# Attention 1 of a fused transformer layer: both diagonal blocks of four heads on the token side, sums copied by ScalarE, products on GpSimd

## The chip, the cores and the metric

The kernel runs on one core of a Trainium2 chip. The metric is device microseconds of that core, median of several runs: 4908.79 us before the change (10 runs, 4905.26 to 4916.34). The core has five engines that each work through their own instructions in order: TensorE (PE; its weight loads are shown as PEld), VectorE (DVE), ScalarE (ACT), GpSimd (POOL) and SyncE (SP). Semaphores order them among each other. DMA transfers are issued here from SP and from POOL.

## The reference, cut to what matters

The layer is an attention over channels, a layer norm, a second attention over the sequence with a mixture of experts, and more norms. The change touches the first attention alone:

```python
Q = (x @ Wq + bq).reshape(b, s, H, C) * inv_sqrt_c      # H = 16, C = 64
K = (x @ Wk + bk).reshape(b, s, H, C)
V = (x @ Wv + bv).reshape(b, s, H, C)
scores = jnp.einsum('bshq,bshk->bshqk', Q, K)
scores = jnp.where(mask, -inf, scores)                   # mask: k > q
w = jax.nn.softmax(scores, axis=-1)
attn = jnp.einsum('bshqk,bshk->bshq', w, V).reshape(b, s, HID) @ Wo + bo
x = _layernorm(x + attn)
```

There are 8 x 1024 = 8192 tokens of 256 features. For each token and head the scores are the outer product of two vectors of 64 numbers, a 64 x 64 square of which the lower triangle counts. A softmax runs along its rows, and the result is multiplied by the 64 values of V. No two tokens meet in it.

## The kernel before, in words

**Tiles and cycles.** `phase_a` works on 64 tiles of 128 tokens. A tile has eight cycles c = 0 to 7: cycles 0 to 3 take the tile's first 64 tokens, 4 to 7 the other 64, and each of the four takes four of the 16 heads. The loop `for t in range(NT + 1)` (L762) writes the instructions of all engines out by hand, cycle by cycle; the dictionaries `between`, `after`, `fill_a` and `fill_b` (L714 to L735) say which work of the tile before ("-"), this one ("") or the next one ("+") is put between the cycle's parts. Each engine keeps that order.

**Scores on PE.** `scores(t, c, which)` (L376) makes score blocks by matmuls over tiles R (q and the row maxima, spread block-diagonally) and L (k and constants), so that a matmul gives q·k minus the row's maximum. `which` 0 and 1 take two heads each: the first 32 columns against all 64 rows. `which` 2 takes all four heads: the last 32 columns against the last 32 rows. Ahead of them four bfloat16 matmuls (L388) put the mask in. Each call fills two PSUM tiles `pair` of 128 x 1024, out of three, and ACT takes their exponential into a tile `e` (L416).

**Sums on PE.** `sums(t, c, which)` (L420) multiplies `e` by V, spread with columns of ones, so that numerators and denominators come out together: L430 for the first 32 columns, L439 for the last 32. Both calls of a cycle use the one PSUM bank `sum`; it is copied to the tile S (L451) by ACT for the first two heads and by DVE for the other two. After every second cycle eight POOL DMAs (L461) carry S to `nd`, which has one row per token.

**The token side.** In cycles 3 and 7, the last four heads, `scores` has no call with `which` 2. The last 32 x 32 block of these heads is done with one token per partition: `token_scores` multiplies k by q on DVE (L497), subtracts the row maximum on POOL (L498) and masks there by affine_select (L500); `token_exp` is on ACT; `token_sums` (L521 to L523) is a row sum, a product with v and another row sum on DVE. The six `pieces` are strips of 8 rows, 256 to 512 elements per partition, one begun in each of cycles 0 to 5 and finished in the next. `token_v` (L465) makes v for it by a projection of its own, at the end of cycle 7.

**Operands.** `extrema` and `maxima` give the row maxima: two running scans of k, two products with q (L343, L344) and a maximum, all on DVE. `build(t, r)` copies q and maxima to R by eight POOL DMAs (L357) and k to L by 16 SP DMAs (L363). It is called in cycles 0, 2, 4 for the pair of cycles after the next, and in cycle 6 for the next tile. There are two R and two L. `gather` writes a one-element `event` on POOL (L371) after waiting for these transfers, and the score matmuls wait for the event.

**After the sums.** `divide` (L525) makes a quarter of the attention output: reciprocal of the denominators (L533) and a product (L534), two quarters in cycle 7 and two in cycle 1 of the next tile; the last adds the token side's part. `turn` transposes it in cycles 4 and 5 of the next tile, `output` multiplies by Wo in cycles 6 and 7, its second half ending with the sum r (L569) on DVE and the norm's statistics. All projections, `turn` and `output` share one PSUM bank `ps`.

The order of one cycle, in the loop:

```python
if live and c < len(pieces):
    token_scores(t, c)
if live:
    scores(t, c, 0 if short else 2)      # short: c % 4 == 3
if c % 2 == 1 and (live and c < 7 or more):
    gather((c + 1) // 2 % 4)
if before is not None:
    sums(*before, 1)
...
if live and c % 2 == 0 and c < 6:
    build(t, c // 2 + 1)
```

then `fill_a`, `scores(t, c, 0)` where the cycle isn't short, `token_exp(t, c - 1)`, `between`, `scores(t, c, 1)`, `sums(t, c, 0)`, `fill_b`, `token_sums(t, c - 1)` and `after`.

## Time and profile before

| | |
|---|---|
| median of 10 runs | 4908.79 us |
| the profiled execution | 4919.86 us, span 4918.1 us |
| TensorE clock granted, mean of the span | 0.982 |
| exponentials of attention 1 (L416), first to last start | 40.1 to 4187.1 us |
| L416, ACT, 128 x 1024 | 2816 times, mean 1021 ns |
| L451, copy of sums by DVE / by ACT | 512 times each, 691 / 592 ns |
| L461 and L357, POOL DMA issues | 2048 times each, 492 and 483 ns |
| L498, POOL subtraction on the token side | 384 times, mean 1009 ns |
| L533, DVE reciprocal | 256 times, 1740 ns |

A row of the profile names the line, the engine, the operation and what it writes and reads, then how often, for how long, and how long the engine was idle before it and what ended that. `s<-k,qm` is the product on the token side, `R<-qm` the fetch of operands, `nd<-S` the way back of the sums. In the order of time each row has its start in us from the span's start and its duration in us; rows of one kind that follow each other are merged (x8). A duration of PE is that of a pipelined matmul: the distance from one start to the next says what it costs.

### The profile page before, as it was taken

What the parts mean: (1) busy time and instruction counts of PE and PEld (TensorE: products, weight loads), DVE (VectorE), ACT (ScalarE), POOL (GpSimd) and SP (SyncE); (2) the same over time, 40 slices, a digit from 0 to 9 for tenths busy, and PEclk for the clock granted to TensorE, in tenths of its full rate; (3) what the DMA queues carried; (4) which work ended last, traced back from release to release, by engine and by line L of the source; (5) the groups of instructions that cost most, each with busy time, mean ns of one, the idle gap of its engine ahead of it and who ended that gap; (6) DMA issues with size and microseconds to landing.
All of it is one profiled execution on the core that took longest, in us unless ns stands there. A gap on an engine that the chain in (4) does not pass through costs nothing.

```text
span 4918.1 us, 173591 instructions
## 1 busy us (share of the span) xinstructions
PE 4691.3 (95%) x70872; PEld 3047.9 (62%) x70872; DVE 3767.6 (77%) x7390; ACT 3503.9 (71%) x4759; POOL 2990.6 (61%) x5670
## 2 busy tenths in 40 slices
PE   8999999999999999999999999999999998888785
PEld 4666666666666666666666666666666665555563
DVE  6777777777777777877777787777777776577778
ACT  5777777777777777777777777777777777444334
POOL 5666666666666666666666666666666665132346
PEclk9999999999999999999999999999999999999987
DMA  2212222221222222212222122222222222133443
GB/s 78 49 48 51 48 49 48 49 50 48 51 50 48 51 47 50 51 47 50 49 48 51 48 50 49 49 51 48 49 49 49 51 49 68 49 77 83 130 150 116
DMA packets 521795, 285.98 MB, mean 58 GB/s; under 512 B 373921, under 2 KB 439841, under 8 KB 520993
## 3 DMA queue, kind: packets, MB, share of 16 engines
q1 hardware_dynamic: 378466, 113.23, 11.8%
q0 software_dynamic: 139264, 159.69, 10.3%
q8 instruction: 554, 9.08, 0.8%
q10 hardware_dynamic: 3264, 1.97, 0.2%
q14 instruction: 247, 2.02, 0.1%
HBM read 72.90 MB, written 33.85 MB: 22 GB/s over the span
## 4 chain that ended last, share of the span: by engine, by line
PE 40%; DVE 7%; ACT 3%; DMA 2%; issue 1%; POOL 1%; SPq 0%; ACTq 0%; POOLq 0%; DVEq 0%
PE pair L400 10%; PE sum L430 9%; PE pair L388 3%; PE sum L439 3%; PE ps L290 2%; PE ps L323 2%; PE ps L279 2%; PE ps L564 2%; ACT s L959 1%; DMA w<-in_w 1%; ACT e L416 1%; PE fill L1017 1%; PE fill L890 1%; PE ps L546 1%; DVE n L1252 1%
## 5 line engine op out<-in xcount | busy, mean ns | idle before, releaser
L416 ACT ACTIVATE e<-pair 128x1024 f32<-128x1024 f32 x2816 | 2729.8, 1021 | 957.1 <-PE pair L400 950.4
L400 PE MATMUL pair<-R,L 32*128 32x128 f32 (+1 forms) x28672 | 1497.9, 332 | 21.6 <-POOL event L371 21.3
L461 POOL DMA_DIRECT2D nd<-S x2048 | 992.4, 492 | 530.5 <-DVE S L451 459.1
L430 PE MATMUL sum<-e,V 128*32 128x256 f32 x16384 | 1241.3, 386 | 13.0 <-ACT S L451 1.8
L400 PEld LDWEIGHTS pair<-R,L 32*128 32x128 f32 x28672 | 1138.8, 186 | 71.5 <-POOL event L371 29.6
L357 POOL DMA_DIRECT2D R<-qm x2048 | 973.2, 483 | 59.3 <-issue 40.4
L451 DVE COPY S<-sum 128x512 f32<-128x512 f32 x512 | 354.0, 691 | 653.2 <-PE sum L439 543.4
L498 POOL TENSOR_TENSOR s<-s,qm 128x512 f32<-128x512 f32 (+2 forms) x384 | 387.6, 1009 | 575.2 <-DVE s L497 572.1
L439 PE MATMUL sum<-e,V 128*32 128x128 f32 x12288 | 617.6, 273 | 0.0
L430 PEld LDWEIGHTS sum<-e,V 128*32 128x32 f32 x16384 | 412.3, 109 | 330.7 <-ACT S L451 74.3
L439 PEld LDWEIGHTS sum<-e,V 128*32 128x32 f32 x12288 | 399.6, 110 | 264.3 <-issue 0.9
L388 PE MATMUL pair<-late,sel 32*128 32x256 bf16 (+1 forms) x5632 | 484.2, 307 | 7.2 <-ACT e L416 7.2
L311 DVE COPY V<-vT 32x128 f32<-32x128 f32 (+1 forms) x2048 | 458.7, 224 | 27.1
L388 PEld LDWEIGHTS <-sel 32*128 32x128 bf16 x5632 | 154.9, 91 | 492.4 <-issue 466.3
L533 DVE RECIPROCAL att<-nd 128x256 f32<-128x256 f32 x256 | 445.5, 1740 | 13.7 <-DMA nd<-S 9.5
L451 ACT COPY S<-sum 128x512 f32<-128x512 f32 x512 | 303.2, 592 | 0.8 <-PE sum L439 0.8
L500 POOL TENSOR_SCALAR_AFFINE_SELECT s<-s 128x128 f32<-128x128 f32 (+1 forms) x384 | 276.1, 719 | 28.2
L279 PE MATMUL ps<-wk,xT 128*128 128x512 f32 x512 | 257.5, 626 | 11.9 <-DMA wk<-in_Wk 10.6
L290 PEld LDWEIGHTS ps<-xT,wv 128*128 128x128 f32 x2048 | 238.2, 191 | 45.3 <-issue 25.8
L290 PE MATMUL ps<-xT,wv 128*128 128x128 f32 x2048 | 262.6, 281 | 1.6 <-DVE qm L324 0.8
L323 PE MATMUL ps<-wq,xT 128*128 128x512 f32 x512 | 257.4, 626 | 5.3 <-DVE k L280 5.3
L564 PE MATMUL ps<-wo,attT 128*128 128x256 f32 x1024 | 255.0, 392 | 0.7 <-ACT attT L547 0.7
(244 smaller groups left out, 5327.5 us busy)
## 6 DMA issues: line engine op xcount, KB each, us to landing
R<-qm POOLq DMA_DIRECT2D x2048, 32.0 KB, 2.2
nd<-S POOLq DMA_DIRECT2D x2048, 32.0 KB, 1.9
L<-k SPq DMA_DIRECT2D x4088, 8.0 KB
rows_d<-yx SPq DMA_DIRECT2D x32, 512.0 KB
xT<-in_xT SPq DMA_DIRECT2D x64, 128.0 KB
xr<-in_x SPq DMA_DIRECT2D x64, 128.0 KB
x_d<-x1o SPq DMA_DIRECT2D x64, 128.0 KB
w<-in_w SPq DMA_DIRECT2D x32, 256.0 KB
```

The costliest lines, as they stand in the source:

```text
L290: nc.tensor.matmul(ps[:, i * P : (i + 1) * P], w["v"][:, c, ch * P : (ch + 1) * P], xT_of[t][:, c, :], start=c == 0, stop=c == DC - 1,)
L311: nc.vector.tensor_copy(V[32 * aa : 32 * aa + 32, :, qd // 2, :, aa, 0:4], src[32 * qd : 32 * qd + 32, :n, ww, :, aa, :],)
L357: moved.append((None, nc.gpsimd.dma_start(R[:, b, s, b, :], q[:, b, s, cols])))
L388: nc.tensor.matmul(bank[u].rearrange("p (n i) -> p n i", i=n)[:, :, 0:32], sel[pr].rearrange("p a j -> p (a j)"), late[pr, None, :].to_bro ...
L400: one = nc.tensor.matmul(bank[u][:, x * 4 * n : (x + 1) * 4 * n].rearrange("p (b i) -> p b i", i=n), Lt[pr, 2 * (h0 + h) + jb].rearrange(" ...
L416: nc.scalar.activation(e, pair[i], AF.Exp)
L430: nc.tensor.matmul(dst[32 * u : 32 * u + 32], Vs[ww][:, h0 + h, u, :], e0[u // 2][:, u % 2, x * 256 : (x + 1) * 256].rearrange("p (b i) -> ...
L439: nc.tensor.matmul(dst[32 * u : 32 * u + 32, :, 32:], Vs[ww][:, H1 + h0 + h, u, :], e1[u // 2][:, u % 2, h * 128 : (h + 1) * 128].rearrang ...
L451: (nc.vector.tensor_copy if which else nc.scalar.copy)(S[:, :, at : at + 2, :].rearrange("p b h i -> p h b i"), ps.rearrange("p (h b i) -> ...
L461: nc.gpsimd.dma_start(tok[:, b, s, (h0 - G) * C1 : (h0 + G) * C1], Sx[:, 4 if s else b, b, :])
L498: nc.gpsimd.tensor_tensor(s, s, m, ALU.subtract)
L533: nc.vector.reciprocal(att[:, cols], nd[:, 1, cols])
```

## The change

In cycles 3 and 7 ("full" now) both diagonal 32 x 32 blocks of the four heads go to the token side, and PE keeps only the square between them, last 32 rows against first 32 columns, which needs no mask: one `scores` call (L411 in the new file) without mask matmuls and one `sums` call of 128-column matmuls for all four heads.

The eight triangles of 32 rows are cut into squares of 16, 8 and 4 and triangles of 4. Five pieces take the place of six: two of squares of 16 (1024 elements per partition each), one of squares of 8 (1024), one of triangles of 4 (1024, masked by adding a constant tile `above` on POOL) and one of squares of 4 (512). They begin in cycles 0, 1, 2, 4 and 5, and each is finished in the cycle after. Their row sums go to `part` and `corner`, and the last quarter of `divide` has four adds in place of one.

All sums are copied from PSUM by ACT. The products of the maxima go to POOL (`products`, in cycles 4 and 5), the maximum stays on DVE, in cycles 5 and 6. `residual_bias` goes to POOL. `token_v` is two transposes of the projected v and an ACT copy, in cycle 6. The tiles `e` are six of a list instead of eight of a pool, S is two fixed tiles, and the scratch of dynamic DMAs is 2048 bytes instead of 4096.

```diff
-    HT, BI = 4, 8
-    pieces = [(0, 0, 4), (1, 0, 4), (2, 0, 2), (2, 2, 2), (3, 0, 2), (3, 2, 2)]
+    HT, BI = 4, 4
+    TC = HT * C1
+    pieces = [(16, 0, 4), (16, 4, 4), (8, 0, 16), (0, 0, 64), (4, 0, 32)]
+    begin = [(0,), (1,), (2,), (), (3,), (4,), (), ()]
+    finish = [(), *begin[:7]]
...
+        def products(t, half):
...
+            nc.gpsimd.tensor_tensor(hi, hi, qm[:, 0, cols], ALU.mult)
+            nc.gpsimd.tensor_tensor(lo, lo, qm[:, 0, cols], ALU.mult)
+
         def maxima(t, half):
...
-            nc.vector.tensor_tensor(hi, hi, qm[:, 0, cols], ALU.mult)
-            nc.vector.tensor_tensor(lo, lo, qm[:, 0, cols], ALU.mult)
             nc.vector.tensor_tensor(hi, hi, lo, ALU.max)
...
-            for u in range(4):
+            full = c % 4 == 3
+            for u in range(0 if full else 4):
...
-            jb = 0 if which < 2 else 1
+            jb = 0 if which < 2 or full else 1
...
-            (nc.vector.tensor_copy if which else nc.scalar.copy)(
-                S[:, :, at : at + 2, :].rearrange("p b h i -> p h b i"),
-                ps.rearrange("p (h b i) -> p h b i", h=2, b=4),
+            n, i0 = (4, 32) if full else (2, 0)
+            nc.scalar.copy(
+                S[:, :, at : at + n, i0:].rearrange("p b h i -> p h b i"),
+                ps.rearrange("p (h b i) -> p h b i", h=n, b=4),
             )
...
+            nc.vector.tensor_tensor(s, k, q, ALU.mult)
+            nc.gpsimd.tensor_tensor(s, s, m, ALU.subtract)
+            if pieces[n][0] == 0:
+                nc.gpsimd.tensor_tensor(s, s, above[:, None, :, :].to_broadcast(shape), ALU.add)
...
+            nc.vector.tensor_reduce(rows[1], s, AX.X, ALU.add)
+            nc.vector.tensor_tensor(s, s, v, ALU.mult)
+            nc.vector.tensor_reduce(rows[0], s, AX.X, ALU.add)
...
-                nc.vector.tensor_tensor(late, late, state["nt", t], ALU.add)
+                own = nd[:, :, cols]
+                nc.vector.tensor_tensor(own, own, corner, ALU.add)
+                for w, p in part.items():
+                    rows = own.rearrange("p s (b z i) -> p s b z i", z=2, i=w)[:, :, :, 1, :]
+                    nc.vector.tensor_tensor(rows, rows, p.rearrange("p s (b i) -> p s b i", i=w), ALU.add)
...
-            nc.vector.tensor_tensor(xr, xr, bo, ALU.add)
+            nc.gpsimd.tensor_tensor(xr, xr, bo, ALU.add)
...
-            4: [("+", maxima, 0)],
-            5: [("+", maxima, 1), ("-", residual_bias)],
-            6: [("+", spread_v, 0, 0)],
+            4: [("+", products, 0)],
+            5: [("+", maxima, 0), ("+", products, 1), ("-", residual_bias)],
+            6: [("+", maxima, 1), ("+", spread_v, 0, 0)],
...
-                short = c % 4 == 3
-                if live and c < len(pieces):
-                    token_scores(t, c)
+                full = c % 4 == 3
+                for n in begin[c][:1] if live else ():
+                    token_scores(t, n)
                 if live:
-                    scores(t, c, 0 if short else 2)
+                    scores(t, c, 2)
...
-                if live and 0 < c <= len(pieces):
-                    token_sums(t, c - 1)
+                for n in finish[c][:1] if live else ():
+                    token_sums(t, n)
...
-    nc = bacc.Bacc("TRN2", target_bir_lowering=False, num_devices=1, dynamic_dma_scratch_size=4096)
+    nc = bacc.Bacc("TRN2", target_bir_lowering=False, num_devices=1, dynamic_dma_scratch_size=2048)
```

## The prediction

> **What bounds the kernel now.** I read the page first, then busy time by window, groups by form, one tile in order of time, and the waits.

> ```profile
> span 4918.1 us, 173591 instructions
> PE 4691.3 (95%) x70872; PEld 3047.9 (62%) x70872; DVE 3767.6 (77%) x7390; ACT 3503.9 (71%) x4759; POOL 2990.6 (61%) x5670
> ...
> 2000.00:3000.00 1000.00, 993.48 (x16384) 639.96 (x16380) 787.20 (x1463) 775.16 (x930) 653.80 (x1272) 1.00 0.21 49
> ```

> The last line is one millisecond inside attention 1: PE 99.3% busy at full clock, DVE 79%, ACT 78%, POOL 65%. TensorE sets the pace. The event ahead of each pair of cycles occurs 124 times from 1013.2 to 2997.9 us, four per tile, so a tile takes 1984.7/123 x 4 = 64.5 us. But one chain that feeds PE has almost no slack, which one tile in order of time shows (start, duration):

> ```profile
> 2043.73 0.41 DVE L569 TENSOR_TENSOR r<-ps,xr 128x256 f32<-128x256 f32 x1
> ...
> 2047.04 0.41 DVE L497 TENSOR_TENSOR s<-k,qm 128x256 f32<-128x256 f32 x1
> ...
> 2063.71 0.55 DVE L497 TENSOR_TENSOR s<-k,qm 128x384 f32<-128x384 f32 x1
> 2064.34 0.84 POOL L498 TENSOR_TENSOR s<-s,qm 128x384 f32<-128x384 f32 x1 [5.56 <-DVE s L497]
> 2065.74 3.84 POOL L461 DMA_DIRECT2D nd<-S  x8
> 2069.57 3.80 POOL L357 DMA_DIRECT2D R<-qm  x8
> ...
> 2076.47 0.09 POOL L371 MEMSET event<- 1x1 f32 x1
> ...
> 2076.82 1.27 PE L400 MATMUL pair<-R,L 32*128 32x128 f32 x32
> ```

> Cycle 2 of this tile starts on PE at 2061.70, cycle 4 at 2076.54. The operands R of cycles 4 and 5 are fetched by POOL in cycle 2, behind the token subtraction of cycle 2, which itself waits for the DVE product k·q at 2063.71. The event comes at 2076.47 and PE's matmuls follow at 2076.82: already now just in time. Whatever makes k·q of cycle 2 later moves the event by as much.

> ```profile
> POOL s L498 <- DVE s L497: 140.9, 46, 5.6
> POOL nd L461 <- DVE S L451: 104.6, 16, 8.8
> POOL event L371 <- DMA R<-qm: 26.1, 17, 3.1
> ```

> Of the waits in the same millisecond (total, times, longest), POOL's largest is for that product, up to 5.6 us.

> **What PE saves.** By start-to-start times, a scores call with 256-column matmuls is 1.09 us, one with 128 columns 1.21 (0.22 of it the mask matmuls), a sums call without a second block 1.00, with it 1.44. Cycles 3 and 7 lose 2 x 1.09 + 2 x 1.00 = 4.18 us and get one unmasked scores call (1.0, the 32-matmul row) and one sums call of 32 matmuls over 128 columns. Eight such take 0.22 to 0.33 us in L439's rows: 0.9 to 1.3, I take 1.0. token_v's projection (0.65) becomes two transposes (0.3, half of four in 0.6). Together 2 x 2.18 + 0.35 = 4.7 us: PE needs 59.8 us a tile, if fed.

> **What the others get.** By these rows of the same millisecond:

> ```profile
> L533 DVE RECIPROCAL att<-nd 128x256 f32<-128x256 f32 x60 | 104.4, 1740 | 0.7
> L498 POOL TENSOR_TENSOR s<-s,qm 128x512 f32<-128x512 f32 x47 | 50.2, 1068 | 41.2 <-DVE s L497 40.7
> L497 DVE TENSOR_TENSOR s<-k,qm 128x512 f32<-128x512 f32 x47 | 32.2, 685 | 0.2
> ...
> L497 DVE TENSOR_TENSOR s<-k,qm 128x256 f32<-128x256 f32 x15 | 6.2, 415 | 0.0
> ```

> - DVE token work: 0.415 at 256 elements, 0.685 at 512, so an estimated 1.22 at 1024; the reduces have the same line (0.411, 0.686). Four operations on 4 x 1024 + 512 elements are 22.3 us against 14.3 now. Three adds more in divide and a wider one: 0.6 + 3 x 0.4 = 1.8 against 0.4. Gone: its eight S copies, 8 x 0.69 = 5.5; four products 2 x (1.07 + 0.81) = 3.8; vt 0.3; xr 0.5. Net -0.7: DVE's total hardly moves, its order does.
> - POOL: 0.63 at 256, 1.07 at 512, so 1.94 at 1024. Subtractions 8.8 against 6.0, the new add 1.9, products 4 x 1.07 = 4.3, xr 0.6, no masks by affine_select (-4.3): +5.3 on 42 us. Products come after R in cycle 4 and after the event in cycle 5, xr behind them; ahead of the next issues that leaves about 3 us free, so I price their place at 0, at most their 2.1 + 2.1 + 0.6 if that cover goes. DVE's maximum in cycle 5 now waits for the first products, some 14 us into cycle 4 (two token operations 3.9, nd 3.95, R 3.8, products 2.1). Behind it on DVE stands the copy that frees the projection bank for the turn; PE has 2.5 us of scores and sums before it wants that bank, which covers the delay: 0, at most 1 us.
> - ACT: four exponentials of 0.97 fewer, six copies of 0.59 more, token exponentials 4.9 (0.82 per 1000 elements and 0.21 fixed, from 420 and 631 ns) against 3.4, vt 0.4: 49.8 becomes about 51.5 of 59.8. A sum's copy now stands behind two exponentials; nd waits for it, but the subtraction holds POOL longer. The token exponential of 1.05 in cycles 1, 2, 3, 5 may hold the sum bank some 0.2 us each: hidden while PE waits anyway, else up to 0.8.
> - SP's L issues and the number of POOL DMAs stay. The DMA scratch is halved: 139264 packets over 4096 transfers are 34 each, and 2.2 us to landing at 0.48 an issue mean about 5 in flight. I take 0; if the half allowed only half of these, issues would space at 0.96 and the 16 in the chain would cost 7.7 us a tile. No row points there.

> **The chain, in us after r** (r waits for the end of output's second half, now the last thing of cycle 7):
> 1. r, statistics, second divide: 3.1 (2107.93 to 2111.04 in the next tile). k·q of cycle 0: 1.2, at 4.3.
> 2. POOL subtraction 1.94, at 6.35; eight nd issues 3.95, at 10.3; landing 1.9, at 12.2. DVE meanwhile: V copies 2.2 + 1.8, k 0.6, k·q of cycle 1, all done by 12.0 even if held 1.9 by the subtraction.
> 3. divide of the third quarter needs that nd: 2.2, at 14.4; second k copy 0.6, at 15.0.
> 4. POOL: eight R to 14.1, subtraction of cycle 1 to 16.05. The four adds of divide's last quarter wait for it (below): 16.05 + 1.8 = 17.85; reciprocal and product 2.2, at 20.05.
> 5. token sums of cycle 1, 3 x 1.22: 23.7. Then only k·q of cycle 2: 24.9. Before, it ended 20.5 after r.
> 6. POOL: subtraction, at 26.95; nd 3.85, R 3.8, at 34.6; landing 2.2 (once 3.5, from 2088.8 to the event at 2092.3), event and PE 0.2: 37.0. Before: 33.1.
> 7. PE from there to the end of output: 8.1 + 8.8 + 8.5 + 4.4 = 29.8 for cycles 4 to 7, and 0.1 to r.

> Sum 66.9 us, a closed loop, against PE's 59.8. PE alone would be there 59.8 - 29.9 = 29.9 us after r, so it waits some 7 us at cycle 4; a second wait, for the event of cycle 0, is 1 to 2 us and hidden by the first. The tile shown took 64.2 (r at 2043.73 and 2107.93), the mean 64.5; with the same 0.3 for what disturbs a tile now and then: 67.2. So +2.7 us on some 63 tiles, +170; the first tile has no divide and saves 4.7. The profiled run took 4919.86, 11 above the median, so 4920 + 165 = 5085 like it and **5075** on the median's scale. DMA landing (1.9 to 3.5) and step 4 bound this loop at 65.6 to 69.5: 4980 to 5225.

> **The lock in step 4.** [...]

> ```profile
> 2088.79 1.67 DVE L343 TENSOR_TENSOR qm<-qm 128x512 f32<-128x512 f32 x1
> ...
> 2088.84 1.06 POOL L498 TENSOR_TENSOR s<-s,qm 128x512 f32<-128x512 f32 x1
> ```

> 1.67 us where L345, of the same size, has 0.69: it ended 0.56 after POOL. The adds would be free at 15.0 and are held to 16.05. [...] Without any lock it would be 1.05 x 63 less, 5010. [...]

> **Rivals.**
> - PE stays the bound (faster). 64 x 4.7 = 301 us less, 4608. For it: the 99.3%. Against it: step 6 would have to end at 29.9, with k·q of cycle 2 done 17.8 us after r, which leaves 5.6 after step 2's landing for steps 3 to 5, whose DVE rows alone are 11.7. Break-even is 64.5 - 29.9 = 34.6 at step 6.
> - The loop is there but shorter by 3 to 6 us (a landing that isn't waited for, shorter wide operations): 60.5 to 64 us a tile, 4660 to 4880.
> - POOL's and DVE's lock or the 4-wide rows cost more: 3 to 5 us on cycles 4 to 7, where DVE has some 0.5 us to spare before r. 70 to 72 us: 5260 to 5390. For it: L343's row; against it: DVE waits for nd there anyway.

> **How the numbers follow.** Loop as summed 0.70 (4980 to 5240), dearer 0.08, shorter loop 0.08, PE-bound 0.11, no change 0.03 (0.2%, 10 us, is about what can be told apart). So slower 0.78, same 0.03, faster 0.19. The range leaves out the PE-bound case, the lower part of the shorter loop and the upper part of the dearer: 4850 to 5250; the likeliest case's own is 4980 to 5225.

> **What would show it.** Tile period near 67; PE waiting some 7 us per tile for the event ahead of cycle 4, PE's share near 89% in the middle; DVE products of 1024 near 1.22, POOL's near 1.94; POOL's longest wait for k·q of cycle 2. Wrong if that event comes before PE gets there, or if 1024-wide rows are far from these.

## The result, and the profile after

The changed kernel takes 5640.17 us (median of 8 runs, 5633.86 to 5658.82) against 4909.23 for the kernel before, run beside it: a ratio of 1.1493 (1.1483 to 1.1503). It is slower, as predicted, but by 731 us, not by 166, and outside the range. By the sums r, of which there is one per tile, a tile took (4208.2 - 164.1) / 63 = 64.19 us before (first and last of them) and (4948.5 - 183.2) / 63 = 75.64 us now: 11.45 more, and 63 times that is 721 of the 731 us. The last of these intervals is short, 20.5 and 21.7 us, since its tile has none after it to prepare; over 32 tiles in the middle the mean is 64.5 us before, which is the prediction's figure, and 76.4 now.

First the page of the kernel after (engine shares, and three groups with their idle time and what ended it):

```profile
PE 4658.0 (82%) x69720; PEld 3131.5 (55%) x69720; DVE 4162.2 (74%) x6430; ACT 3567.3 (63%) x4887; POOL 3425.5 (61%) x5609
...
L411 PE MATMUL pair<-R,L 32*128 32x128 f32 (+1 forms) x28672 | 1494.3, 340 | 550.4 <-POOL event L381 550.2
...
L355 DVE TENSOR_TENSOR qm<-qm,lo 128x512 f32<-128x512 f32 x128 | 302.4, 2363 | 290.6 <-POOL lo L350 290.6
...
L577 PE MATMUL ps<-wo,attT 128*128 128x256 f32 x1024 | 305.8, 450 | 156.0 <-ACT vt L485 155.4
```

No engine leads any more. TensorE lost 550 us to the event, which the prediction had, and 155 us in front of the output's matmuls to an ACT copy, which it hadn't. The maximum L355 is an operation of 0.68 us that took 2.36 on average. The waits in the millisecond shown for the kernel before, 2000 to 3000 us (total, times, longest):

```profile
POOL s L509 <- DVE s L508: 164.7, 38, 10.1
PE pair L411 <- POOL event L381: 112.3, 15, 8.9
PE ps L577 <- ACT vt L485: 32.5, 13, 2.5
PE ps L554 <- DVE vT L303: 18.6, 11, 3.3
```

Times 75.64 us a tile these are 8.5, 2.5 and 1.4 us a tile of TensorE's waiting, 12.4 together. Busy time by windows in the same millisecond (length, busy time and instructions of PE, PEld, DVE, ACT and POOL, granted clock, DMA share, GB/s):

```profile
2000.00:3000.00 1000.00, 835.35 (x13706) 560.67 (x13702) 743.97 (x1047) 672.58 (x817) 644.17 (x1062) 0.92 0.16 42
```

TensorE is busy for 0.835 x 75.64 = 63.2 us a tile, where 59.8 were worked out for its work, and the clock granted is 0.92 where it was 1.00. So the tile is some 60 us of work, 3 us by which the same work took longer, and 12.4 us of waits. The three stalls in order of time, first those of cycles 5 and 6 (start, duration; in brackets the idle time before and what ended it):

```profile
2003.46 1.10 POOL L509 TENSOR_TENSOR s<-s,qm 128x512 f32<-128x512 f32 x1
2003.55 4.72 DVE L355 TENSOR_TENSOR qm<-qm,lo 128x512 f32<-128x512 f32 x1 [5.02 <-POOL lo L350]
...
2004.55 1.27 POOL L349 TENSOR_TENSOR qm<-qm 128x512 f32<-128x512 f32 x1
...
2005.78 1.26 POOL L350 TENSOR_TENSOR lo<-lo,qm 128x512 f32<-128x512 f32 x1
...
2007.01 0.71 POOL L564 TENSOR_TENSOR xr<-xr,bo 128x256 f32<-128x256 f32 x1
2008.20 0.68 DVE L303 TENSOR_TENSOR vT<-ps,bv 128x512 f32<-128x512 f32 x1
...
2008.93 1.12 PE L554 MATMUL ps<-ident,att 128*128 128x128 f32 x4 [2.59 <-DVE vT L303]
...
2014.69 0.44 PE L483 MATMUL ps<-ident,vT 128*128 128x128 f32 x2
...
2014.86 1.94 ACT L426 ACTIVATE e<-pair 128x1024 f32<-128x1024 f32 x2
...
2016.68 0.63 ACT L516 ACTIVATE s<-s 128x512 f32<-128x512 f32 x1
...
2017.20 0.37 ACT L485 COPY vt<-ps 128x256 f32<-128x256 f32 x1
...
2017.63 2.61 PE L577 MATMUL ps<-wo,attT 128*128 128x256 f32 x8 [2.50 <-ACT vt L485]
```

The maximum waits for POOL's products, then stays held under four POOL operations that follow each other, until 2008.2. The copy that frees the bank `ps` stands behind it on VectorE, and the turn waits for that. In cycle 6 the output's first half waits for ScalarE to copy the turned v out of the other half of the bank that it writes, and ScalarE does so behind two exponentials of the scores and one of the token side. Then the stall of cycle 4 in the next tile, from the r ahead of it to its own:

```profile
2028.36 0.42 DVE L582 TENSOR_TENSOR r<-ps,xr 128x256 f32<-128x256 f32 x1 [5.62 <-PE ps L577]
...
2053.13 1.22 DVE L508 TENSOR_TENSOR s<-k,qm 128x1024 f32<-128x1024 f32 x1
...
2054.50 2.02 POOL L509 TENSOR_TENSOR s<-s,qm 128x1024 f32<-128x1024 f32 x1 [8.98 <-DVE s L508]
...
2056.45 3.84 POOL L475 DMA_DIRECT2D nd<-S  x8
...
2060.29 3.80 POOL L367 DMA_DIRECT2D R<-qm  x8
...
2066.10 0.09 POOL L381 MEMSET event<- 1x1 f32 x1 [2.01 <-DMA L<-k]
2066.24 2.09 PE L411 MATMUL pair<-R,L 32*128 32x128 f32 x32 [7.71 <-POOL event L381]
...
2095.54 1.99 PE L577 MATMUL ps<-wo,attT 128*128 128x256 f32 x8 [2.50 <-ACT vt L485]
...
2104.70 0.42 DVE L582 TENSOR_TENSOR r<-ps,xr 128x256 f32<-128x256 f32 x1 [4.83 <-PE ps L577]
```

The product ends 26.0 us after r (24.9 predicted) and the event comes 37.7 after it, with PE at 37.9 (37.0 predicted): the chain up to the event is as summed. (The event's row names an L transfer as the last to land; those for cycles 4 and 5 were issued from 2042.98 to 2054.36, long before, so it is the R transfers that count.) But the 32 matmuls behind the event take 2.09 us, at a granted clock of 0.50, where this row has 1.06 in cycles without a wait ahead, and from there to the next r it is 38.5 us, where the prediction has 29.9.

### The profile page after: what moved, and what is told of

Its sections match the earlier page's. It is cut to its first block, busy times and chain, and to the rows that moved or that the text cites. A ratio compares the mean times of both kernels' runs of the same rounds, so it can differ in the third digit from the quotient of the medians.

```text
span 5655.3 us, 168921 instructions
## 1 busy us (share of the span) xinstructions
PE 4658.0 (82%) x69720; PEld 3131.5 (55%) x69720; DVE 4162.2 (74%) x6430; ACT 3567.3 (63%) x4887; POOL 3425.5 (61%) x5609
## 3 DMA queue, kind: packets, MB, share of 16 engines
q0 software_dynamic: 139264, 159.69, 9.0%
## 5 line engine op out<-in xcount | busy, mean ns | idle before, releaser
L426 ACT ACTIVATE e<-pair 128x1024 f32<-128x1024 f32 x2560 | 2483.8, 1023 | 1512.0 <-PE pair L411 1475.6
L411 PE MATMUL pair<-R,L 32*128 32x128 f32 (+1 forms) x28672 | 1494.3, 340 | 550.4 <-POOL event L381 550.2
L411 PEld LDWEIGHTS pair<-R,L 32*128 32x128 f32 x28672 | 1169.5, 203 | 643.8 <-POOL event L381 578.5
L509 POOL TENSOR_TENSOR s<-s,qm 128x1024 f32<-128x1024 f32 (+1 forms) x320 | 574.8, 1796 | 798.5 <-DVE s L508 742.6
L441 PE MATMUL sum<-e,V 128*32 128x256 f32 x12288 | 977.0, 390 | 0.7 <-ACT S L465 0.5
L453 PE MATMUL sum<-e,V 128*32 128x128 f32 x16384 | 809.3, 291 | 0.0
L317 DVE COPY V<-vT 32x128 f32<-32x128 f32 (+1 forms) x2048 | 553.3, 270 | 27.2
L465 ACT COPY S<-sum 128x512 f32<-128x512 f32 x896 | 531.3, 593 | 10.1 <-PE sum L453 10.1
L355 DVE TENSOR_TENSOR qm<-qm,lo 128x512 f32<-128x512 f32 x128 | 302.4, 2363 | 290.6 <-POOL lo L350 290.6
L441 PEld LDWEIGHTS sum<-e,V 128*32 128x32 f32 x12288 | 307.6, 110 | 188.1 <-issue 138.1
L527 DVE TENSOR_TENSOR s<-s,vt 128x1024 f32<-128x1024 f32 (+1 forms) x320 | 360.0, 1125 | 11.1
L508 DVE TENSOR_TENSOR s<-k,qm 128x1024 f32<-128x1024 f32 (+1 forms) x320 | 355.1, 1110 | 3.1
L577 PEld LDWEIGHTS ps<-wo,attT 128*128 128x128 f32 x1024 | 213.9, 219 | 214.3 <-ACT vt L485 170.1
```

Source lines behind the costliest of these rows:

```text
L317: nc.vector.tensor_copy(V[32 * aa : 32 * aa + 32, :, qd // 2, :, aa, 0:4], src[32 * qd : 32 * qd + 32, :n, ww, :, aa, :],)
L411: one = nc.tensor.matmul(bank[u][:, x * 4 * n : (x + 1) * 4 * n].rearrange("p (b i) -> p b i", i=n), Lt[pr, 2 * (h0 + h) + jb].rearrange(" ...
L426: nc.scalar.activation(es[i], pair[i], AF.Exp)
L441: nc.tensor.matmul(dst[32 * u : 32 * u + 32], Vs[ww][:, h0 + h, u, :], e0[u // 2][:, u % 2, x * 256 : (x + 1) * 256].rearrange("p (b i) -> ...
L453: nc.tensor.matmul(dst[32 * u : 32 * u + 32], Vs[ww][:, (0 if full else H1) + h0 + h, u, :], e1[u // 2][:, u % 2, h * P : (h + 1) * P].rea ...
L465: nc.scalar.copy(S[:, :, at : at + n, i0:].rearrange("p b h i -> p h b i"), ps.rearrange("p (h b i) -> p h b i", h=n, b=4),)
```

## The experiments

All ratios are to the kernel before, run beside the kernel in question. "Tile" is the mean from r to r over the whole run. The last three columns are TensorE's waits, in us a tile, worked out from the waits between 2000 and 3000 us, for the event, in front of the turn, and in front of the output. Left out are 0.7 to 0.8 us a tile that it waits for r, in the kernels that turn v behind the output.

| kernel | us | ratio (95%) | tile | event | turn | output |
|---|---|---|---|---|---|---|
| before | 4909.23 | 1 | 64.19 | 0.2 | - | - |
| after | 5640.17 | 1.1493 (1.1483, 1.1503) | 75.64 | 8.5 | 1.4 | 2.5 |
| late_subtraction | 5804.01 | 1.1807 (1.1787, 1.1827) | 77.82 | 1.8 | 11.2 | 2.3 |
| products_on_dve | 5552.70 | 1.1301 (1.1282, 1.1320) | 74.09 | 8.7 | - | 2.4 |
| v_turned_last | 5404.84 | 1.0998 (1.0974, 1.1021) | 71.59 | 7.6 | 1.4 | - |
| three_waits | 5125.99 | 1.0433 (1.0415, 1.0450) | 67.42 | 3.2 | 2.2 | - |
| sum_copies_on_dve | 5885.10 | 1.1984 (1.1964, 1.2004) | 79.11 | 4.4 | 4.3 | 2.6 |
| dve_products_busy_pe | 5376.69 | 1.0946 (1.0928, 1.0964) | 71.32 | 1.7 | - | 2.5 |
| two_of_three | 5394.96 | 1.0989 (1.0970, 1.1007) | 71.48 | 2.9 | 3.0 | 2.5 |
| late_products | 5213.63 | 1.0617 (1.0599, 1.0635) | 68.74 | 5.0 | 0.9 | - |
| no_token_work | 5027.26 | 1.0151 (1.0131, 1.0170) | 65.10 | 1.3 | 1.4 | 1.9 |
| no_token_no_waits | 4825.97 | 0.9830 (0.9815, 0.9845) | 62.71 | 1.9 | - | - |
| loop_alone | 5286.24 | 1.0759 (1.0741, 1.0777) | 69.76 | 7.5 | - | - |
| loop_alone_busy_pe | 5172.25 | 1.0524 (1.0506, 1.0541) | 68.09 | 0.9 | - | - |
| before_v_turned | 4896.76 | 0.9969 (0.9959, 0.9979) | 63.83 | 0.2 | - | - |

**POOL's subtraction of cycle 2 behind the R issues.** My first theory was the predicted loop, with its event as the place to cut.

```diff
             nc.vector.tensor_tensor(s, k, q, ALU.mult)
-            nc.gpsimd.tensor_tensor(s, s, m, ALU.subtract)
+            state["s", t, n] = flat, s; state["m", t, n] = m
+            if n not in (2,): token_lower(t, n)      # POOL's part
...
                     build(t, c // 2 + 1)
+                for n in begin[c][:1] if live else ():
+                    if n in (2,): token_lower(t, n)
```

> One step of the changed kernel is moved: in cycle 2 POOL subtracts the maximum of the token side after it has issued nd and R, not before. The changed kernel stands at 5640 us and about 76 us a tile. Theory A (the loop of the prediction: k·q of cycle 2 on DVE, subtraction, nd, R, event, PE): the event ahead of cycle 4 is then set by the ACT copy of the sums, 4.2 + 3.9 + 3.8 + 2.2 = 14 us after the start of cycle 2, where PE arrives after 12.6, so 7.7 us of waiting become some 1.5 and the slow clock behind it goes too: 66 to 68 us a tile, 5000 to 5130 us. Theory B (DVE and POOL have too much work between them, and the wait only shows where it ends last): it comes back at the next event or at r, over 72 us a tile, above 5350 us.

It got slower by 164 us. The event's wait went, as it should, and all of it and more came back at the turn:

```profile
2046.68 1.27 POOL L350 TENSOR_TENSOR qm<-qm 128x512 f32<-128x512 f32 x1
2047.90 1.26 POOL L351 TENSOR_TENSOR lo<-lo,qm 128x512 f32<-128x512 f32 x1
...
2049.20 4.71 DVE L356 TENSOR_TENSOR qm<-qm,lo 128x512 f32<-128x512 f32 x1 [8.44 <-POOL lo L351]
...
2053.83 0.68 DVE L304 TENSOR_TENSOR vT<-ps,bv 128x512 f32<-128x512 f32 x1
2054.57 1.11 PE L563 MATMUL ps<-ident,att 128*128 128x128 f32 x4 [11.30 <-DVE vT L304]
```

So there is a second chain of nearly the same length: POOL reaches the products only behind its nd and R issues, the maximum waits for them, the freed bank for the maximum, the turn for the bank. TensorE gets to cycle 5 earlier now, and waits there 11.3 us instead of 2.6.

**The products back on VectorE.** The edit is two lines, `nc.gpsimd` to `nc.vector`, in `products`.

> The four products of the maxima go back to DVE, their place stays. [...] Theory B: 2.7 us more on DVE make k·q and the sums later by as much, no gain or a loss: 5600 to 5750 us.

87 us fewer, where theory B had no gain and my own estimate, from a wait of 2.6 us a tile and about 1 of slow clock behind it, was 190 to 250; the wait in front of the turn is gone. Alone, the second chain is worth 1.55 us a tile.

**The turned v behind the output.** `token_v` moves from in front of the output's first half, in cycle 6, to behind its second half, in cycle 7; the bank is the same.

```diff
             ps = state["pv"] = pps.tile([P, 512], FP, name="ps")
-            if t + 1 < NT:
-                token_v(t + 1, ps)
             if 0 < t <= NT:
                 output(t - 1, 0)
+        def output_end(t):
+            if 0 < t <= NT: output(t - 1, 1)
+            if t + 1 < NT: token_v(t + 1, state["pv"])
```

> The two transposes of v and their ACT copy move from ahead of output's first half in cycle 6 to behind its second half in cycle 7, in the same bank. Theory A: PE doesn't wait 2.5 us in cycle 6 for the copy, nor run some 1.5 us longer at the lower clock after it: 3.5 to 4 us a tile less, 5390 to 5420 us. Theory B: the wait is not on the loop, and PE waits as much longer for the event ahead of cycle 4: 5620 to 5660 us.

235 us fewer, as theory A had it, and 4.05 us a tile: the largest single term of the miss. The wait of 2.5 us goes, the event's falls by 0.9, and a new one of 0.7 appears, since the turned v now stands behind r's reading of the bank. The remaining 1.3 us are fewer busy us of TensorE (0.835 x 75.64 against 0.865 x 71.59): the output's matmuls, 16 a tile, fell from 448 to 392 ns each. Why they were slow is asked below.

**All three, and two of them.**

> The three edits together. Theory A: the loop is open, PE is the bound again with 60 to 62 us a tile and little waiting: 4620 to 4750 us, faster than before the change. Theory B: DVE, some 58 of 60 us busy then, keeps PE waiting: 64 to 67 us a tile, 4880 to 5070 us.

> The changed kernel with POOL's subtraction of cycle 2 behind the R issues and the products on VectorE, but with the turned v still ahead of the output. Alone, the first cost 164 us and the second won 87. Theory A (two closed loops of nearly one length: one over k*q of cycle 2 and the event, one over the products on POOL, the maximum and the turn; each edit opens one of them): together they win more than either, 5330 to 5420. Theory B (the effects add up): 5640 + 164 - 87 = 5717, at least over 5600.

The three edits together win 514 us, less than either theory had (5126 against at most 5070), and stay above the kernel before. The pair came out as its theory A had it, and settles the two chains: the late subtraction costs 2.2 us a tile while the products are on POOL (75.64 to 77.82) and wins 2.6 once they aren't (74.09 to 71.48).

**The sums' copies back on VectorE.** One line, for the second call of each cycle: `(nc.vector.tensor_copy if which else nc.scalar.copy)`.

> Undoes one small part of the change alone: the copies of S for the second query block go back from ScalarE to VectorE, as the kernel before had them. Three such copies (0.69 us each in the kernel before) then stand on VectorE between r and k*q of cycle 2. Theory A (VectorE's work between r and k*q of cycle 2 is on the loop, that is why the copies were moved): 1 to 2 us a tile longer, 5640 becomes 5700 to 5770. Theory B (ScalarE's copies stand behind two exponentials and hold nd, so VectorE is the better place): nd earlier by 1 to 2 us, 5510 to 5600.

245 us more, past both expectations. The waits show why it isn't the copies' own 0.69 us:

```profile
PE pair L411 <- POOL event L381: 55.3, 24, 3.9
PE ps L554 <- DVE vT L303: 54.9, 13, 7.5
PE sum L441 <- DVE S L465: 40.8, 12, 3.9
```

A new one, the last of these rows, is 3.2 us a tile: TensorE waits for the only bank of sums, because VectorE gets to the copy late. The turn's wait grew from 1.4 to 4.3. This part of the change is a gain in its new surroundings.

**Does TensorE run slower after a wait?** 32 useless matmuls fill the wait ahead of cycle 4.

```diff
+            for i in range(32 if c == 4 and which == 2 else 0):
+                nc.tensor.matmul(bank[i % 4], sel..., late[:, None, :].to_broadcast([P, 16, 32]),
+                                 start=True, stop=True, skip_group_check=True)
```

> The changed kernel with the products on VectorE (5553 us) and 32 useless matmuls of 512 columns into the pair banks ahead of the scores of cycle 4, where TensorE waits some 9 us for the event; the scores write over them, so the output stays the same. They are work added for nothing. Theory A (after such a wait TensorE is granted a lower clock for some 4 us, which costs about 1.8 us a tile on the loop): the waiting time is filled, the groups after the event take 1.1 us instead of 2.1, and 63 x 1.8 = 113 us go: about 5440. Theory B (the slow groups after the event are slow for another reason, operands for example): they stay near 2 us and the time is 5553 or, where the useless matmuls outlast the wait, more, up to 5650.

176 us fewer, by adding work, and 63 more than expected: the output's matmuls, 16 a tile, fell from 507 to 440 ns each as well, 1.1 us a tile. Busy time by windows of 3.41 us, first the kernel without the useless matmuls (TensorE idle from 2005.86 to 2013.25, the work behind that wait, and the output's wait, 2037.3 to 2039.8, with its first half behind it), then, in other windows, with them (the useless matmuls, and the stretch behind the event):

```profile
2005.62:2009.03 3.41, 0.23 (x4) 0.00 (x0) 3.41 (x5) 0.00 (x1) 3.41 (x8) 1.00 0.31 85
2009.03:2012.44 3.41, 0.00 (x0) 0.00 (x0) 3.34 (x4) 0.00 (x0) 2.18 (x5) 0.50 0.29 75
2012.44:2015.86 3.42, 2.61 (x44) 2.36 (x48) 3.42 (x4) 0.43 (x1) 2.17 (x2) 0.50 0.19 48
2015.86:2019.27 3.41, 3.41 (x49) 2.15 (x41) 0.78 (x1) 2.00 (x3) 3.33 (x3) 0.50 0.01 2
2019.27:2022.68 3.41, 3.41 (x44) 2.81 (x48) 1.38 (x2) 2.17 (x3) 3.41 (x9) 1.00 0.21 62
...
2036.34:2039.75 3.41, 0.98 (x14) 0.40 (x6) 2.68 (x13) 3.30 (x6) 2.51 (x6) 1.00 0.20 47
2039.75:2043.17 3.42, 3.35 (x8) 2.52 (x8) 2.25 (x4) 0.02 (x1) 3.42 (x8) 0.50 0.31 81
```

```profile
2015.80:2022.60 6.80, 6.80 (x33) 3.01 (x31) 6.73 (x7) 0.24 (x1) 4.87 (x11) 1.00 0.29 73
2022.70:2026.40 3.70, 3.70 (x90) 2.78 (x89) 3.42 (x3) 2.23 (x3) 3.11 (x3) 1.00 0.16 42
```

The granted clock (third column from the end) falls to 0.50 3.2 us after TensorE went idle and is back at 2019.27, 6.0 us after the work began again; with the wait filled the stretch behind the event runs at 1.00. The output's eight matmuls take 3.63 us, nearly all at 0.50, where they take 1.99 at full clock. The window ahead of them was not idle: TensorE was busy for 0.98 of its 3.41 us.

In the kernel after, every change of the clock lies at a whole number of 3.41 us from every other. Between 1000 and 3500 us, each of the 65 such windows that had the full clock and came before a lowered one was busy for at most 0.48 of its length, each of the 540 before another full one for at least 0.43, so the two overlap; after a lowered window the clock came back when it had been busy for at least 0.83 (65 windows) and stayed low up to 0.85 (62). In the kernel before, the one window ahead of a lowered one in that stretch was busy for 0.59. What a wait cost went by where it fell in these windows too: after the same 2.50 us, at 2095.54 in the kernel after, the output's eight matmuls took 1.99 us at a clock of 1.00, and that wait lay across two windows, busy for 2.49 and 1.84 us. That is the likely reason why filling one wait sped the output's matmuls up as well, whose own wait stayed at 2.5; that is inferred.

**The first products in cycle 5**, behind the copy that frees the bank, in the kernel without the three waits:

> The kernel with all three waits removed (5126 us), and in it the first two products moved on VectorE from cycle 4 to cycle 5, behind the vT copy that frees the turn's bank. Theory A (the 2.3 to 2.5 us that TensorE still waits for that copy in cycle 5 go, and VectorE has room for the products before the maximum): 1.5 to 3 us a tile less, 4920 to 5040. Theory B (VectorE, 88.5 per cent busy, is the bound by now and only the order changes, or the maximum comes later and the next R with it): 5080 to 5200.

88 us more, just past theory B. The turn's wait fell from 2.2 to 0.9 us and the event's rose from 3.2 to 5.0, so one was given for the other; that the later maximum delays the next R, as B had it, I infer from that.

**The product of cycle 0 ahead of r, and v's copy by ScalarE.** Both go on top of the three edits.

> The kernel with the three waits removed (5126 us), and in it the product k*q of cycle 0 moved to cycle 7 of the tile before, ahead of r, where VectorE waits for TensorE and for the division's data; POOL's subtraction of it goes along. Theory A (the loop over the event is still what sets the pace, and this takes 1.2 us of VectorE and 1.9 of POOL out of it): 2 to 3 us a tile less, 4940 to 5000. Theory B (VectorE's and POOL's sum of work, lock included, sets the pace, so that only the order changes): 5080 to 5160.

> The kernel before it, with the copy of the projected v (0.69 us, twice a tile, VectorE) done by ScalarE in four pieces of 128 columns each, with the bias added. TensorE's turn waits 2.3 us a tile for this copy in cycle 5, because VectorE is held by POOL there. Theory A (that wait is on the path): 1.5 to 3 us a tile less than the kernel before it, so 4780 to 4900 if that one falls as far as theory A of it says, else 4940 to 5030. Theory B (ScalarE's 2 to 3 us more a tile delay the exponentials and the copies of S, which nd waits for): no gain, or up to 1.5 us a tile more.

Neither won: 1.0409 (1.0392, 1.0426), about the 1.0433 without it, and 1.0519 (1.0500, 1.0538), where the turn's wait is gone and the event's rose from 3.3 to 5.6 us a tile; the kernel before took 4954.73 us beside these two and no_token_work, so of the three only the ratios compare. **Useless matmuls** (six each ahead of cycles 0 and 4) don't help there either:

> The kernel with the three waits removed (1.0433 of the kernel before), with six useless matmuls of 512 columns (1.3 us) ahead of the scores of cycle 0 and of cycle 4, where TensorE still waits 1.6 to 2.8 us for the event; work added for nothing, the output stays the same. Theory A (the granted clock still falls after these waits, mean 0.97, and filling them keeps it): 1 to 2 us a tile less, 1.018 to 1.032. Theory B (the waits there are too short to cost clock, or the loop is VectorE's and TensorE's clock is off the path): 1.038 to 1.060.

1.0477 (1.0459, 1.0495): the event's wait halved, 3.2 to 1.5 us a tile, and the tile stayed at 67.38. What closes the loop at 67.4 us isn't settled; VectorE, busy there for 885 of 1000 us with its waits under POOL's operations counted in, is the nearest, and no run shows it.

**Is TensorE's saving real?** The token work is left out, first alone, then with the products on VectorE and v turned last.

```diff
+        for p in (corner, *part.values()): nc.vector.memset(p, 1.0)
         def token_scores(t, n):
+            return                  # the same in token_exp and token_sums
```

> The changed kernel without its token work: the products k*q, POOL's subtractions and the add, the token exponentials, their sums and products with v are left out (the partial sums are set to 1 once), so its output isn't the reference's. All else stays: fewer matmuls, products on POOL, copies by ScalarE, adds in the divide. Theory A (the wide token operations on VectorE and POOL make both loops; without them TensorE is fed and needs its own 59.8 us a tile): 4610 to 4730. Theory B (the other moves, products on POOL and the turned v ahead of the output, cost by themselves, through the lock and the bank): 64 us a tile or more, over 4880.

> The changed kernel without its token work, as before (output not the reference's), and with the products back on VectorE and v turned behind the output's second half. With the token work out alone it still took 1.015 of the kernel before. Theory A (what is left of the loss there is the products on POOL and the bank shared by the turned v and the output; TensorE's own need is the 59.8 us a tile that was worked out, 4.7 less than before): 0.935 to 0.955 of the kernel before, 4590 to 4690. Theory B (TensorE's saving is smaller, or another wait, the nd issues behind ScalarE's copies, holds it): 0.965 or more, over 4740.

Without any token arithmetic the kernel is still 1.5% slower than the one before, which falsifies theory A of that run; with the two waits out as well it is 1.7% faster, but not the 4.5 to 6.5% that its theory A had; its theory B holds. Its millisecond:

```profile
2000.00:3000.00 1000.00, 957.76 (x16498) 638.80 (x16491) 492.16 (x1015) 738.51 (x903) 513.06 (x1126) 0.99 0.20 50
```

TensorE is busy for 0.958 x 62.71 = 60.1 us a tile, against the 59.8 worked out, and against 0.993 x 64.19 = 63.8 before. So 3.7 of the 4.7 us show at a clock of 0.99; at 1.00, in loop_alone_busy_pe below, it is 0.976 x 68.09 less 7.07 of useless matmuls, 59.4, and 4.4. Most of the saving is there, and 1.9 us of event and 0.7 of r a tile still stand before it. POOL waits for ScalarE's copies of S ahead of the nd issues for 307.6 us of that millisecond; that this is what holds the event isn't shown.

**The predicted loop by itself.** The subtraction in its place, products on VectorE, v turned last; then the same with the 32 useless matmuls.

> The changed kernel with the products on VectorE and v turned behind the output, POOL's subtraction of cycle 2 in its own place: the loop of the prediction by itself, without the two waits in cycles 5 and 6 that it hadn't. Theory A (the prediction's loop is right but for the clock after its wait: 66.9 worked out, 0.3 for what disturbs a tile, 0.7 by which the event came later than worked out, 1.8 for slow matmuls after the wait): 69.7 us a tile against 64.2 before, ratio 1.06 to 1.08. Theory B (other waits take their place, the loop isn't understood): 1.09 or more.

> The same with 32 useless matmuls of 512 columns ahead of the scores of cycle 4, where TensorE waits some 7 us for the event; work added for nothing. Theory A: only the clock's 1.8 us go, 67.2 to 67.9 us a tile, ratio 1.035 to 1.05, 2 to 2.5 per cent under the kernel before it, and the mean granted clock at 0.99. Theory B (the clock matters only in chains with two stalls): within 1 per cent of the kernel before it.

The first came out at 69.76 us a tile, 69.7 expected, the second at 68.09 and 1.0524, a little above its 67.2 to 67.9 and 1.035 to 1.05. First the loop alone, from the event to r; then with the wait filled:

```profile
2046.27 0.09 POOL L381 MEMSET event<- 1x1 f32 x1 [2.37 <-DMA L<-k]
...
2078.09 0.42 DVE L586 TENSOR_TENSOR r<-ps,xr 128x256 f32<-128x256 f32 x1 [1.06 <-PE ps L581]
```

```profile
2066.89 7.07 PE L398 MATMUL pair<-late,sel 128*128 128x512 bf16 x32
2073.55 0.09 POOL L381 MEMSET event<- 1x1 f32 x1 [1.90 <-DMA L<-k]
2074.12 1.06 PE L420 MATMUL pair<-R,L 32*128 32x128 f32 x32
...
2104.26 0.42 DVE L595 TENSOR_TENSOR r<-ps,xr 128x256 f32<-128x256 f32 x1 [0.36 <-PE ps L590]
```

From event to r it is 31.8 us instead of the 30.1 of the prediction (its last step and 0.2 from the event to PE). Filling the wait takes 1.67 us off the tile, and from PE's start to r it is then 30.1, against 29.9 predicted.

**One part alone, in the kernel before:** vt by two transposes, copied by ScalarE, at the end of cycle 7. The bank is still the one `ps`, but in a turn of its own, where the expectation calls it a bank of their own.

```diff
             ps = pps.tile([P, 512], FP, name="ps")
-            for c in range(DC): nc.tensor.matmul(ps[:, : HT * 32], xT_of[t][:, c, :], w["v"]...)
+            for i in range(2): nc.tensor.transpose(ps[:, i * P : (i + 1) * P], state["vT", t][:, HID // P - 2 + i, :], ident)
-            nc.vector.tensor_tensor(state["vt", t], ps..., bv_row, ALU.add)
+            nc.scalar.copy(state["vt", t], ps...)
```

> One part of the change alone, in the kernel before: vt comes from two transposes of the projected v, copied by ScalarE, in a bank of their own, in place of its own projection and VectorE's add. Theory A (TensorE is the bound there, so its 0.35 us a tile are gained; the bank isn't shared with the output): 22 us less, ratio 0.994 to 0.998. Theory B (the transposes wait for ScalarE or the bank stays taken longer, in front of the next projection): ratio 1.000 to 1.02.

With all of the token work in place it is the one version faster than both kernels: 4896.76 us, 0.9969 (0.9959 to 0.9979), 0.36 us a tile, as worked out for that part.

## Why the prediction was wrong in size

From before over loop_alone_busy_pe, loop_alone and v_turned_last to after, the 11.45 us a tile split into four terms. That they add up follows from how they are taken; each of them is measured.

| term | from | us a tile |
|---|---|---|
| the predicted loop, wait filled | loop_alone_busy_pe - before, 68.09 - 64.19 | 3.90 |
| slow clock after the event's wait | loop_alone - loop_alone_busy_pe | 1.67 |
| products on POOL | v_turned_last - loop_alone, 71.59 - 69.76 | 1.83 |
| turned v ahead of the output | after - v_turned_last, 75.64 - 71.59 | 4.05 |

Taken in the other order the last two are 1.55 and 4.33, so they interact by no more than 0.3.

- *What PE saves.* Right within 0.3 us a tile: 4.4 at full clock against 4.7.
- *The chain, steps 1 to 6.* Right within 1 us: PE starts 37.9 us after r against 37.0; rows of 1024 elements 1.22 on VectorE and 1.97 on POOL against 1.22 and 1.94. Of the 1.1 us by which k·q of cycle 2 is late, most comes from step 3, where POOL's subtraction of cycle 1 already holds the product of the third quarter (2.86 us at 2041.76, 0.42 elsewhere), an operation earlier than step 4 has it. The 1.05 us for which step 4 has the subtraction hold the adds was an estimate from one row of L343, and no run shows it as a term of the tile: in the kernel after, three of the four adds (L540) took 0.42 to 0.43 us all 192 times, and the first (L537) 0.68 at the median and 2.50 at most. The forecast of 67.2 us a tile stands against 68.09 for this loop with the wait filled, or 68.7 in the middle of the run, where before has the 64.5 that the forecast starts from. The direction and its reason, TensorE losing its lead to the loop over k·q of cycle 2, nd, R and the event, hold.
- *The chain, step 7, "PE from there to the end of output: 29.8".* This is the step that failed: 38.5 us in the tile shown. It was made of cycles at full clock and without waits, and so it holds where the wait is filled and the other two are gone (30.1). In its place: 1.67 us of lowered clock after the event, two more waits of 1.4 and 2.5 us, and again a lowered clock after those (in the rows of cycles 5 and 6, 0.50 from 2008.63 to 2012.04 and from 2018.87 to 2022.28). I had forecast a 7 us wait and never asked at what clock TensorE comes out of one. The millisecond that I read, 99.3% busy, holds no such wait, but the same trace does further on, after the first attention, with TensorE busy for 153.56 of 200 us at a clock of 0.88:

```profile
4500.00:4700.00 200.00, 153.56 (x868) 107.39 (x867) 153.45 (x367) 64.67 (x230) 71.45 (x94) 0.88 0.41 109
```

- *What the others get, "DVE's maximum in cycle 5 now waits for the first products: 0, at most 1 us".* Wrong: 1.55 to 1.83. The delay up to the products was seen; that the maximum, once started, would take 4.7 us under four POOL operations instead of 0.68 was not, though the prediction showed the lock one operation deep. VectorE's total, which was to hardly move, rose from 0.787 x 64.19 = 50.5 to 0.744 x 75.64 = 56.3 us a tile, the time held under POOL counted in.
- *token_v as two transposes for 0.3 us.* The price of the matmuls was right (before_v_turned gains the 0.36). What was left out is a term: the bank. The output's first matmul writes the bank that ScalarE is still to read, behind three exponentials. 4.05 to 4.33 us, the largest miss. The two halves of the bank don't overlap; whether the wait is needed, no run shows.
- *ACT 51.5 us, POOL +5.3.* 0.673 x 75.64 = 50.9, and 48.7 against 42.0, so +6.7; neither decides. Copies by ScalarE are not neutral but good: 3.5 us a tile worse without.
- *The scratch of DMAs, halved: 0.* Eight issues took 3.80 to 3.84 us, as before, and landed in 1.8 at the median, where the kernel before has 2.2 (R) and 1.9 (nd); nothing points there. It wasn't tried alone, nor was the bias on POOL or the other layout of `e` and S.
- *Rivals.* "PE stays bound" is out. The dearer loop, through the lock, was the right direction with 8 in 100 and still 250 us too low, since it had neither the clock nor the bank in it. (The likeliest case's own range is given as 4980 to 5225 and as 4980 to 5240; neither reaches 5640.)
- *Signs.* The wait of some 7 us (7.71), the rows of 1024 elements and POOL's longest wait, for k·q, came as forecast; the tile near 67 us and PE's share near 89% (83.5%) did not.

## What to carry to other kernels

A single shared buffer (a PSUM bank, here) is part of a chain: for each operation put into it, ask who must read it out before the next writer, and what stands ahead of that reader in its engine's queue. When a change makes a busy TensorE wait, price the time behind the wait at the lower clock, here 6.0 us of work at 0.50 after a wait of 7.4, not only the wait. And cut chains together, since another of like length stands behind the one that the profile shows: here one cut alone cost 164 us and won 158 with the next chain open (5552.70 to 5394.96).
